# Planned times of TensorE's transposes and products in a two-layer decoder

## The chip, the cores and the metric

The kernel runs on one core of one Trainium2 chip. The metric is the device time of one execution in microseconds (us), of which the median of several runs is taken. A core has TensorE (PE in the profile; its weight loads are PEld), VectorE (DVE), ScalarE (ACT), GpSimd (POOL) and SyncE (SP), which here issues direct DMAs. Each engine works through its own queue in order.

## The reference

Everything is float32. The input x is 16 sequences of 256 tokens with 256 channels: 4096 tokens. Six sublayers follow each other, and each adds to x what it computes from the layer-normalised x:

```python
x = x + _L0_attn_ref(_layernorm(x), ...)           # causal linear attention, 16 heads of 16
x = x + _L0_xattn_ref(_layernorm(x), ctx_1024, ...)  # softmax attention to 77 context rows
x = x + _L0_ffn_ref(_layernorm(x), ...)            # 16 experts, top 2 of a sigmoid router
x = x + _L1_attn_ref(_layernorm(x), ...)           # 8 heads, keys and values of a 64-wide latent
x = x + _L1_xattn_ref(_layernorm(x), ctx_1024, ctx_1024, ..., mask_SxS2_ik0)
x = x + _L1_ffn_ref(_layernorm(x), ...)            # gated, with quantised weights and activations
```

The expert layer gives each expert 640 rows at most and gathers the results of a token's two experts with the router's weights.

## The kernel before, in words

The 4096 tokens are 32 tiles of 128 rows; x stays on chip in 32 tiles of 128x256. Tiles are worked in groups ("batches") of four. The profile shows five stages one after another.

1. `l0_attention` (L520), 0 to 275 us of the span: projections, score products ps_sc, products with the masked scores la_at, and the output product with Wo (ps_av<-w_L_attn_WoT,la_aT).
2. `l0_cross` (L1035), to about 573: for each tile, `scores(i)` makes two pairs of score products (ps_sc). For each pair DVE adds the bias into lx_s and takes the maximum lx_mx, POOL or ACT subtracts it, and ACT takes exponentials. `weighted(i)` transposes the weights (ps_pt, four 128-wide ones twice and then two of 104 columns) and copies them to lx_sT and lx_sL. It multiplies them with the values (ps_rec<-lx_sT,lx_v), scales the result by the reciprocal sums (DVE, lx_aT, L1160) and applies Wo (ps_rec<-w_L_xattn_wo,lx_aT), which DVE adds to x. The scores of tile i+1 are written in the program ahead of the weighted sums of tile i. In between stand the query projections of the batch after next (hT, ps_pr), the keys and values of later batches (ps_k, ps_v), and the expert router of the batch before: the normalised rows rh by ACT, their transposes ps_rt (L832), the logits ps_logit (L839), the top two by DVE, the ranks ps_rank (L879), and scatters of the rows into moe_x by POOL's indirect DMAs.
3. `l0_experts` (L1700), to about 893: products ps_h and ps_y with each expert's weights.
4. `l1_tokens` (L1314), to about 1345: POOL gathers the expert results (ex_yg) by indirect DMA. Then both attentions of layer 1 follow for each tile: scores in two halves of four products, exponentials sa_e, multiplication by the reciprocal sums on POOL, 16 transposes ps_pt, products ps_av with the latent and ps_po.
5. `l1_ffn` (L1920), to the end.

Stages 1 to 4 are not issued in the order of the program text. `planned(E)` (L369) puts a `Plan` in the place of the engines. Each operation is recorded as a `Call` with a planned duration in ns (`busy`) and a delay until its readers may start (`tail`). At the end of a stage, `Plan.issue()` (L149 on) works out an order by list scheduling: of the operations whose inputs are ready in the plan, those that could begin within 150 ns (`near`) of the earliest on an engine compete, and the first in program order (`rank`, shifted where the program says urgent) is taken. A copy made with `nc.copy` goes to VectorE or ScalarE, whichever would finish it first in the plan. TensorE is charged an extra 25 to 205 ns between groups of products that use parts of its rows or columns (`CHANGE`). Then all operations are issued, sorted by planned begin, so that each engine's queue has the planned order; on the chip semaphores enforce what must wait. In the profile every planned operation has line L363, that of `Call.issue`. Stage 5 is not planned and its instructions show lines of their own.

The planned durations are set in `Call.__init__` from the number n of elements in a partition: VectorE 50 + 1.05n (with a tail of 140), ScalarE's copies 45 + 0.83n and activations 170 + 0.73n, POOL by kind (an indirect DMA 1250). TensorE's are the lines that the change touches. A float32 product shows as two matmul records in the profile and a transpose as one.

Of the kernel before, what the change touches and what calls it, by code (L numbers as in the profile page):

```python
# [53 lines left out]
class Plan:  # L54
# [17 lines left out]
    def __init__(self, tc, near=150):  # L72
        self.tc, self.nc, self.near = tc, tc.nc, near
        self.ops, self.tiles, self.open, self.shift = [], {}, None, 0
        self.start, self.gate = 0.0, None
        for name in ("tensor", "vector", "scalar", "gpsimd", "sync"):
            setattr(self, name, Engine(self, name))
# [211 lines left out]
def region(ap):  # L289

    if ap.space == DRAM:
        return ap.tensor.name, 0, 1, 0, 1
    step, rows = ap.ap[0]
    row, first = divmod(ap.offset, step)
    if ap.space == PSUM:
        return ap.tensor.name, row, row + rows, first // 512, first // 512 + 1 + (free(ap) - 1) // 512
    reach = sum(s * (n - 1) for s, n in ap.ap[1:])
    return ap.tensor.name, row, row + rows, first, first + reach + 1


def free(ap):
    n = 1
    for _, k in ap.ap[1:]:
        n *= k
    return n


class Call:
# [3 lines left out]
    def __init__(self, nc, engine, method, args, kwargs, together=False):  # L312
        self.engine, self.method = engine, method
        self.then, self.loose = kwargs.pop("then", None), kwargs.pop("loose", False)
        self.nc, self.args, self.kwargs = nc, args, kwargs
        named = dict(kwargs)
        out = named.pop("out", None)
        rest = list(args)
        if out is None:
            out = rest.pop(0)  # L320
        extra = named.pop("accum_out", None)
        writes = [out] + ([extra] if extra is not None else [])
        reads = []
        for v in rest + list(named.values()):
            if isinstance(v, bass.IndirectOffsetOnAxis):
                v = v.ap
            if isinstance(v, bass.AP):
                reads.append(v)
        self.kind = "all"
        self.writes, self.reads = [region(w) for w in writes], [region(r) for r in reads]  # L330
        n = max(free(a) for a in writes + reads)
        if engine == "tensor":
            self.busy, self.tail = 2 * max(110, 0.84 * free(out)), 220
            if method == "transpose":
                self.busy = max(60, 0.85 * free(out))
            left = reads[0]
            self.part = (left.offset // left.ap[0][0], out.offset // out.ap[0][0])
            if together:
                self.kind = "row" if left.ap[0][1] <= 64 and out.ap[0][1] == P else "col"
        elif engine == "vector":  # L340
            self.busy, self.tail = 50 + 1.05 * n, 140
            if method == "reciprocal":
                self.busy = 145 + 6.35 * n
        elif engine == "scalar":
            self.busy, self.tail = 45 + 0.83 * n, 165
            if method == "activation":
                self.busy = 170 + 0.73 * n + (92 if extra is not None else 0)
        elif method == "indirect_dma_start":
            self.busy, self.tail = 1250, 2000
        elif method == "dma_start":  # L350
            self.busy, self.tail = 60, 2500
        else:
            even = any(s == 0 for r in reads for s, _ in r.ap[1:])
            self.busy, self.tail = (100 + 1.75 * n if even else 200 + 2.0 * n), 95
            if ALU.pow in args:
                self.busy = 970
            elif method == "tensor_scalar":
                self.busy = 50 + 1.2 * n
            elif method == "tensor_copy":
                self.busy = 110 + 1.0 * n  # L360
# [1791 lines left out]
```

## Time and profile before

| what | value |
| --- | --- |
| runs | 1731.65, 1732.46, 1735.03 us; median 1732.46 |
| profiled execution | 1689.03 us, its span 1687.3 us, mean TensorE clock 0.973 |
| TensorE (matmul, weight load) busy | 1555.7 us, 1034.2 us |
| VectorE, ScalarE, GpSimd busy | 1114.1, 769.5, 450.4 us |
| DMA moved | 92.02 MB, mean 55 GB/s |

The busy time of an engine is the union of its instructions' times. A row of a group reads: line, engine, operation, output<-inputs, shapes, count | busy time, mean ns of one | idle time of the engine just ahead of these, and what ended most of it. A window's row reads: the stretch in us from the span's start, its length, then busy time and number of instructions for PE, PEld, DVE, ACT and POOL, the granted TensorE clock (1 is full), the share of DMA engines busy, and GB/s. A row of the waits reads: what waited, for what: us in total, how many times, the longest. A row of a timeline has the start, the length and the instruction (x4: four in a row), with idle time ahead of it in brackets. The profiled execution is shorter than the median of the runs: 1732.46 / 1689.03 = 1.0257.

### The profile page before, as it was taken

How to read it: one execution, taken by the hardware profiler on the slowest of the kernel's cores; microseconds unless marked ns; L12 is line 12 of the kernel's file. 1: busy time of each engine (PE TensorE's matmuls, PEld its weight loads, DVE VectorE, ACT ScalarE, POOL GpSimd, SP SyncE). 2: the span in 40 equal slices, each digit the busy share in tenths (PEclk: the TensorE clock that was granted, in tenths of full speed). 3: DMA queues.
4: the chain of work that ended last, by engine and by line, in shares of the span. 5: the costliest groups of instructions: out<-in, count | busy, mean ns of one | idle time of the engine just before them, and what ended most of it. 6: DMA issues, size and time to landing. Idle time of an engine off the chain costs nothing.

```text
span 1687.3 us, 24347 instructions
## 1 busy us (share of the span) xinstructions
PE 1555.7 (92%) x9072; PEld 1034.2 (61%) x9072; DVE 1114.1 (66%) x2209; ACT 769.5 (46%) x2017; POOL 450.4 (27%) x521
## 2 busy tenths in 40 slices
PE   5999999998997799999997899999999599999799
PEld 3666665665665677777775666666666344433387
DVE  7988886999997442221126788777757543999951
ACT  4333324767767211111113645554555343667850
POOL 5332212355444200000006887343343100000000
PEclk9999999999998899999998999999999799999899
DMA  6024003011111543344312121000000000001111
GB/s 191 1 97 154 1 1 78 16 48 38 34 37 46 169 131 113 112 126 142 115 61 59 51 63 39 1 1 1 1 1 1 0 0 0 25 37 51 38 50 50
DMA packets 95785, 92.02 MB, mean 55 GB/s; under 512 B 32487, under 2 KB 85439, under 8 KB 95667
## 3 DMA queue, kind: packets, MB, share of 16 engines
q1 hardware_dynamic: 89522, 73.91, 14.4%
q0 software_dynamic: 6144, 16.57, 3.1%
q8 instruction: 71, 1.16, 0.3%
q14 instruction: 48, 0.39, 0.1%
HBM read 52.70 MB, written 36.70 MB: 53 GB/s over the span
## 4 chain that ended last, share of the span: by engine, by line
PE 56%; DVE 26%; issue 7%; ACT 7%; DMA 2%; POOL 2%; SPq 1%; POOLq 0%; ACTq 0%; DVEq 0%
PE ps_y L363 7%; PE ps_h L363 7%; PE ps_pr L363 6%; PE ps_av L363 6%; PE ps_gate L486 5%; PE ps_out L486 5%; PE ps_sc L363 4%; PE ps_pt L363 3%; ACT lx_s L363 3%; PE ps_v L363 2%; PE ps_po L363 2%; DVE x L363 2%; DVE lx_mx L363 2%; DVE ff_g L2015 2%; DVE sa_top L363 2%
## 5 line engine op out<-in xcount | busy, mean ns | idle before, releaser
L363 DVE COPY ex_y<-ps_y 128x256 f32<-128x256 f32 x80 | 33.7, 424 | 217.1 <-PE ps_y L363 217.1
L363 POOL DMA_INDIRECT ex_yg<-moe_y,slot x64 | 64.1, 1002 | 337.5 <-DMA moe_y<-ex_y 320.3
L363 POOL TENSOR_TENSOR sa_e<-sa_e,sa_rec 128x1024 f32<-128x1024 f32 x64 | 121.5, 1906 | 121.3 <-PE ps_pt L363 71.3
L486 PE MATMUL ps_up<-ff_x,ffn_up 128*128 128x512 f32 x336 | 147.0, 595 | 7.1 <-DVE ff_pu L1886 4.3
L363 ACT ACTIVATE sa_e<-ps_sc,sa_top 128x256 f32<-128x256 f32 x256 | 118.2, 485 | 72.1 <-DVE sa_top L363 69.9
L363 PE MATMUL ps_y<-w,ex_h 128*128 128x256 f32 x640 | 141.5, 379 | 4.1 <-DVE ex_y L363 4.1
L363 PE MATMUL ps_h<-ex_xT,w 128*128 128x320 f32 x512 | 143.4, 438 | 0.5 <-ACT ex_h L363 0.5
L363 PEld LDWEIGHTS ps_y<-w,ex_h 128*128 128x128 f32 x640 | 121.4, 190 | 23.3 <-DVE ex_y L363 5.3
L363 ACT ACTIVATE ex_h<-ps_h 128x640 f32<-128x640 f32 x64 | 45.0, 704 | 187.0 <-PE ps_h L363 187.0
L363 PEld LDWEIGHTS ps_h<-ex_xT,w 128*128 128x128 f32 x512 | 96.6, 192 | 40.4 <-ACT ex_h L363 1.0
L486 PEld LDWEIGHTS ps_up<-ff_x,ffn_up 128*128 128x128 f32 x336 | 63.0, 190 | 91.0 <-issue 72.9
L363 ACT ACTIVATE lx_s<-lx_s,lx_mx 128x77 f32<-128x77 f32 x288 | 98.9, 347 | 8.4 <-DVE lx_mx L363 4.7
L486 PE MATMUL ps_out<-ffn_down,ff_g 128*128 128x256 f32 x384 | 84.8, 384 | 11.6 <-issue 11.6
L486 PE MATMUL ps_gate<-ff_x,ffn_gate 128*128 128x512 f32 x192 | 85.0, 606 | 6.5 <-DVE ff_x L1988 6.5
L486 PEld LDWEIGHTS ps_out<-ffn_down,ff_g 128*128 128x128 f32 x384 | 74.1, 193 | 22.7 <-issue 12.4
L363 DVE TENSOR_REDUCE sa_top<-ps_sc 128x4 f32<-128x1024 f32 x64 | 76.4, 1215 | 17.1 <-PE ps_sc L363 16.8
L363 DVE TENSOR_TENSOR la_at<-ps_sc,la_tri 128x1024 f32<-128x1024 f32 x64 | 75.8, 1215 | 8.9 <-PE ps_sc L363 8.8
L363 POOL DMA_INDIRECT moe_x<-rh,slot x64 | 63.7, 995 | 41.9 <-issue 14.3
L363 PE MATMUL ps_pt<-ident,sa_e 128*128 128x128 f32 x512 | 66.9, 281 | 5.9 <-ACT ff_x L363 1.9
L363 PE MATMUL ps_sc<-sa_latT,sa_q 64*128 64x256 f32 x512 | 69.9, 399 | 2.3 <-ACT sa_e L363 2.3
L486 PEld LDWEIGHTS ps_gate<-ff_x,ffn_gate 128*128 128x128 f32 x192 | 37.3, 195 | 53.7 <-issue 53.0
L363 PEld LDWEIGHTS ps_pt<-ident,sa_e 128*128 128x128 f32 x512 | 58.9, 144 | 15.1 <-issue 3.2
(301 smaller groups left out, 3402.3 us busy)
## 6 DMA issues: line engine op xcount, KB each, us to landing
w<-in_L_ffn_w SPq DMA_DIRECT2D x32, 512.0 KB
moe_x<-rt_zero SPq DMA_DIRECT2D x16, 640.0 KB
ex_xg<-moe_x SPq DMA_DIRECT2D x15, 640.0 KB
moe_y<-ex_y SPq DMA_DIRECT2D x15, 640.0 KB
x<-in_x SPq DMA_DIRECT2D x32, 128.0 KB
out_x<-x SPq DMA_DIRECT2D x32, 128.0 KB
ff_u<-ff_c SPq DMA_DIRECT2D x6, 512.0 KB
ff_c<-ff_u SPq DMA_DIRECT2D x6, 512.0 KB
```

Source lines behind the costliest of these rows:

```text
L363: made = getattr(getattr(self.nc, self.engine), self.method)(*self.args, **self.kwargs)
L486: E.nc.tensor.matmul(ps, a, b, start=n == 0, stop=n == last)
L2015: nc.vector.scalar_tensor_tensor(gp, low16(gq, I16), sg16, low16(sig, U16), ALU.mult, ALU.mult)
```

## The change

Three numbers in the planned durations of TensorE change. A product is planned at twice max(112, 0.84 times its width) plus 12 ns where it was twice max(110, 0.84 times its width); a transpose at max(70, 1.1 times its width) where it was max(60, 0.85 times its width).

```diff
         if engine == "tensor":
-            self.busy, self.tail = 2 * max(110, 0.84 * free(out)), 220
+            self.busy, self.tail = 2 * max(112, 0.84 * free(out)) + 12, 220
             if method == "transpose":
-                self.busy = max(60, 0.85 * free(out))
+                self.busy = max(70, 1.1 * free(out))
```

Both kernels issue the same operations; the number of instructions on each engine stays within a few, as copies can change between VectorE and ScalarE. Compared as lists, 875 lines of TensorE's order differ, 1625 of VectorE's, 492 of ScalarE's and 406 of GpSimd's; SyncE's is the same. What the order of instructions shows of the places, beside the prediction's steps:

- Stage 2: in batches two to five the two score pairs of a tile stand one behind the other ahead of the two 104-wide transposes, where one pair stood there and one later; one of two 512-wide query projections goes ahead of the weighted sums; ps_rank goes ahead of Wo. The copies of hT: 13 on ScalarE and 1 on VectorE before, 4 and 10 after. Of lx_sT: 40 and 24 before, 49 and 15 after.
- Stage 4: 81 of 128 copies of sa_eT were on ScalarE, now 87; the gathers ex_yg at the stage's start stand in other places among GpSimd's multiplications.
- Stages 1 and 3: orders change, no copy changes its engine.

## The prediction

> **What bounds the kernel now.** I read the page first, then windows cut at the stage borders, then TensorE's waits, then single timelines.
>
> ```profile
> PE 1555.7 (92%) x9072; PEld 1034.2 (61%) x9072; DVE 1114.1 (66%) x2209; ACT 769.5 (46%) x2017; POOL 450.4 (27%) x521
> PE 56%; DVE 26%; issue 7%; ACT 7%; DMA 2%; POOL 2%; SPq 1%; POOLq 0%; ACTq 0%; DVEq 0%
> L363 PE MATMUL ps_pt<-ident,sa_e 128*128 128x128 f32 x512 | 66.9, 281 | 5.9 <-ACT ff_x L363 1.9
> ```
>
> TensorE is busy 92% of the span, yet only 56% of the chain that ended last is its own: a quarter runs over VectorE. The third row matters for the change: a transpose has a mean of 281 ns, but the union of 512 of them is 66.9 us, 131 ns each. Next, the five stages, and five stretches of them:
>
> ```profile
> 0.00:275.00 275.00, 253.61 (x2248) 163.55 (x2248) 223.68 (x343) 99.92 (x195) 83.13 (x127) 0.99 0.24 73
> 275.00:573.00 298.00, 259.01 (x2269) 178.40 (x2270) 255.36 (x728) 201.80 (x791) 134.96 (x190) 0.95 0.17 45
> 573.00:893.00 320.00, 312.89 (x1364) 242.66 (x1365) 81.04 (x178) 53.82 (x82) 1.00 (x2) 0.99 0.39 122
> 893.00:1345.00 452.00, 413.54 (x2282) 275.22 (x2280) 329.51 (x695) 231.10 (x775) 229.53 (x199) 0.96 0.07 19
> ...
> 330.00:500.00 170.00, 157.43 (x1399) 105.85 (x1398) 157.06 (x440) 119.43 (x452) 87.49 (x123) 0.99 0.16 41
> ...
> 980.00:1270.00 290.00, 284.34 (x1568) 184.75 (x1567) 217.47 (x463) 152.14 (x512) 139.71 (x116) 0.99 0.05 14
> ```
>
> The columns after the length are TensorE, weight loads, DVE, ACT, POOL, clock. TensorE idles 21.4 us in stage 1 (linear attention), 39.0 in stage 2 (cross attention), 7.1 in stage 3 (experts), 38.5 in stage 4 (layer 1 attentions); all that an order can win is in there. In the middle of stage 2 TensorE and DVE are equally full (157.4 and 157.1 of 170), so each waits for the other; in the middle of stage 4 TensorE alone is full (284 of 290). The waits of stage 2:
>
> ```profile
> PE ps_rec L363 <- DVE lx_aT L363: 9.6, 11, 2.1
> PE ps_xT L363 <- DMA ex_xg<-moe_x: 8.5, 1, 8.5
> PE ps_rt L363 <- ACT rh L363: 4.6, 2, 4.2
> ...
> PE ps_pt L363 <- ACT lx_sT L363: 2.9, 4, 0.8
> ```
>
> The costliest is the output product (Wo) of a token tile, which waits for DVE's lx_aT.
>
> **The change, part by part.** No instruction is added or removed. Planned costs of TensorE go up: a 128-wide transpose from 108.8 to 140.8 ns (max(60, 0.85·128), max(70, 1.1·128)), a product by 12 to 16 ns (256 wide: 430 to 442). What happens on the chip is a new order, and some copies on the other engine. Are the new figures nearer the trace?
>
> ```profile
> 1105.76 0.59 PE L363 MATMUL ps_pr<-hT,sa_aq 128*128 128x512 f32 x1
> 1106.18 1.91 PE L363 MATMUL ps_pt<-ident,sa_e 128*128 128x128 f32 x16
> 1107.98 0.48 PE L363 MATMUL ps_cv<-cx_v,cx_eT 77*128 77x256 f32 x1
> ```
>
> From the first of 16 transposes to the instruction behind them is 1.80 us, 112.5 ns each. The Trainium skill ("TensorE: Matmul & The Clock Gate", PE-mode transpose) gives about 275 ns for a 128x128 transpose in a kernel, which this trace's mean of 281 ns repeats; by that figure even 141 is short, 16 would hold TensorE 4.4 us, and the change would be a step to the truth. By the row they hold it 1.80 us, because they overlap; the planner adds its costs end to end, so the cadence is what it needs, and 108.8 was within 4% of it while 140.8 is 25% above. I take the row. For products the old figures also fit: four 256-wide ones started 1.73 us before what follows them (432 each), two 512-wide ones 1.72 us (860). So TensorE is now planned too slow, while DVE stays planned too fast (a 616-wide add at 50 + 1.05·616 = 697 ns against 790 in the trace). The plan thinks that DVE is further ahead than it is.
>
> Stage 2, five full batches of four tiles. A batch lasted 34.7 us (from router logits to router logits: 36.2, 34.9, 34.9, 34.3, 33.4). Before, around one of the Wo products:
>
> ```profile
> 428.60 0.60 PE L363 MATMUL ps_pt<-ident,lx_s 128*128 128x128 f32 x4
> 430.03 0.43 PE L363 MATMUL ps_pt<-ident,lx_s 128*104 128x128 f32 x2 [0.83 <-ACT lx_sT L363]
> ...
> 431.69 1.98 PE L363 MATMUL ps_pr<-hT,w_L_xattn_wq 128*128 128x512 f32 x4
> 433.73 1.13 PE L363 MATMUL ps_rec<-w_L_xattn_wo,lx_aT 128*128 128x256 f32 x4
> ```
>
> - The score pairs move ahead of the two 104-wide transposes and cover that 0.83 (seen three times: 0.5 a batch). The Wo at the batch's end moves behind the 8 transposes of rh and covers its wait for lx_aT (2.10, 1.46 and 0.49 us in three batches: 0.8 a batch). A third, between the last two transposes, covers 0.2.
> - Against it: with the two score pairs so early, DVE has two pairs of add and maximum ahead of lx_aT where it had one: 2 · 0.79 = 1.6 us later. TensorE is there earlier, as one of the two 512-wide products (0.86) now stands ahead of the weighted sums, and the waits of this stretch grow from about 1.1 to about 3.1 us: +2.0 a batch. Behind this Wo in TensorE's queue stand the next tile's transposes, all idle for that time; DVE waits for nobody meanwhile. The rh transposes, reached before the Wo, wait 0.5 for ACT.
> - Nine of 14 hT copies and three of lx_sL move to DVE, thirteen others from DVE to ACT: DVE's load changes by about −1 us over the stage. I cost this at nothing, as ACT has 50 of 170 us free; if DVE is late by one 0.69 us copy at each batch, it is +0.7 a batch.
>
> Sum: 2.0 + 0.5 − 0.5 − 0.8 − 0.2 = +1.0 a batch, +5 over five. Bounds: no new Wo wait, −1.5 a batch (−7.5); all of it and the copy, +1.7 (+8.5). At the stage's end a Wo goes behind both score pairs instead of between them; its tile ends about 1 us later, but ACT's exponentials feed the next step anyway: +0.5 (−0.5 to +1.5).
>
> Stage 1: in seven places the Wo product goes ahead of the scores instead of behind. It saves a change of row grouping (this Wo takes 1.06 us behind scores, 0.86 to 0.90 elsewhere: −0.2) and waits for la_aT about as long (+0.2). 0, between −2 and +2. Stage 3: only weight and input transposes swap, TensorE at 98%: 0 ± 1.
>
> Stage 4: in five places the first half of a tile's score products moves from between transposes to its second half (one change less: −0.2 each, −1.0). Their softmax is needed a tile later, some 8 us, which hides it; without that cover each would cost up to a scores-to-exponentials delay of 1 to 2 us. At the start (893 to 980, TensorE 71.9 of 87, POOL 68.8) POOL's gathers of expert results move ahead of softmax multiplications; a gather is 1.0 us of POOL, so two or three of them make these 2 to 3 us later, and the tiles that need the gathers earlier by the same. No row shows which is late next; I take +1 between −3 and +4. SP's queue is the same. Stage 5 is not planned: 0.
>
> Total: 5 + 0.5 + 0 + 0 − 1 + 1 = +5.5 us on the profiled execution of 1689.03 (span 1687.3), 1694.5. The median of the runs is 1732.46, 1.0257 times that; scaled, 1738.1 us.
>
> **Rivals.** *The covered waits win.* The Wo wait behind the logits stays at its old length, because TensorE gets there later than I walked it; then a batch gains 1.5 and stage 4 one: −8.5, 1680.5, scaled 1723.7. For it: those waits are in the table. Against: DVE is as full as TensorE, so a wait covered here comes back there. It decides at a Wo wait that grows by less than 1.0 us a batch.
> *All is hidden.* Order changes, DVE's 157 us a stretch stay, and each batch ends when DVE does: 1732.5, within 3. For it: equal loads. This is also the case that the change doesn't do what it says, as the new costs are no nearer.
> *DVE and POOL both late.* +8.5 in stage 2, +1.5 at its end, +4 at the start of stage 4, +2 in stage 1: +16, scaled 1748.9. For it: POOL and DVE each have an underestimated plan; against: four ends at once.
>
> **How the numbers follow.** My forecast (+2 to +10 profiled, likeliest 1738.1) 0.46; hidden 0.26; waits win 0.19; both late 0.09. A measurement of this kernel can tell about 0.2%, 3.5 us, from no change. Most of the forecast and the last rival lie above it, the edges go to "same": faster 0.18, same 0.29, slower 0.53. The range runs from 1725 (short of the winning case's centre) to 1750 (the late case): the part outside is at most half of the first rival and of the last.
>
> **What would show it.** In the trace after: the wait of ps_rec for lx_aT grows from 9.6 to some 16 us with single waits of 2 us or more behind ps_rank, while ps_pt's wait for ACT lx_sT falls under 1; the batches last 35 to 36.5 us; stage 4's middle stays at 290 less one; stages 3 and 5 keep their lengths. I am wrong if the batches come under 34 us, or if the difference sits at the start of stage 4.

## The result, and the profile after

The changed kernel takes 1778.68 us (median of 4 runs, 1772.77 to 1788.86); beside it the kernel before takes 1732.06. The ratio is 1.0257, 95% interval 1.023 to 1.0284: 2.6% slower, where 1738.1 was forecast. The profiled execution took 1773.76 us, its span is 1772.0. Of the page and of windows cut at its own stage borders, the lines that answer to those of before:

```profile
PE 1584.8 (89%) x9072; PEld 1047.1 (59%) x9072; DVE 1110.9 (63%) x2203; ACT 772.1 (44%) x2023; POOL 450.9 (25%) x521
...
PE 52%; DVE 26%; issue 8%; ACT 8%; another core or an unknown queue 3%; DMA 2%; POOL 1%; SPq 0%; POOLq 0%; ACTq 0%; DVEq 0%
```

```profile
0.00:278.00 278.00, 256.36 (x2250) 164.68 (x2250) 224.38 (x344) 100.05 (x195) 84.59 (x129) 0.99 0.23 72
278.00:643.00 365.00, 277.65 (x2268) 189.51 (x2268) 254.18 (x726) 202.31 (x792) 134.38 (x187) 0.86 0.14 37
643.00:962.00 319.00, 312.08 (x1358) 241.87 (x1359) 80.93 (x178) 53.06 (x81) 0.05 (x1) 0.99 0.38 123
962.00:1430.00 468.00, 422.30 (x2287) 276.78 (x2286) 327.03 (x690) 233.94 (x781) 230.11 (x200) 0.96 0.07 19
1430.00:1772.00 342.00, 316.43 (x912) 174.24 (x912) 224.43 (x266) 182.78 (x175) 1.79 (x5) 0.97 0.09 31
```

Stage 2 has grown from 298 to 365 us and stage 4 from 452 to 468; the others keep their lengths within 3 us. DVE does the same work in stage 2 (254 us), in a longer time. Most of the growth there is one kind of wait, which TensorE's table names only at second hand (ps_rec for lx_aT, 46.4 us). ScalarE's waits in stage 2, and the timelines of TensorE and ScalarE at the first of them, show it:

```profile
ACT lx_rT L363 <- remote: 56.3, 7, 11.8
```

```profile
338.28 0.38 PE L363 MATMUL ps_rec<-lx_sL,lx_v 104*32 104x128 f32 x2
...
336.03 0.59 ACT L363 COPY lx_sT<-ps_pt 128x512 f32<-128x512 f32 x1
348.46 0.37 ACT L363 COPY lx_rT<-ps_rec 128x256 f32<-128x256 f32 x1 [11.84 <-remote]
```

The copy lx_rT needs what TensorE wrote into ps_rec, and the last of those products had started before 338.6. The copy starts at 348.5, and the profile knows no releaser ("remote"). I call waits without a known releaser freezes. This profile has one more of VectorE (x, 4.2 us); the profile of before has none. Each of the eight begins while GpSimd issues the scatters of a batch (the first at 336.6; scatters from 334.5 to 346.3). In three of the sets of runs below the kernel before takes 1690, and no profile has a freeze; in two others, as in the runs above, it takes 1732 to 1741, and every profile of a kernel that issues the scatters has them. One chip was met in both conditions. So the two profiles shown of before and after come from different conditions, while the ratio of 1.0257 is of runs side by side.

### The profile page after: what moved, and what is told of

It reads as the page before. It is cut to its first block, busy times and chain, and to the rows that moved or that the text cites. A ratio compares the mean times of both kernels' runs of the same rounds, so it can differ in the third digit from the quotient of the medians.

```text
span 1772.0 us, 24370 instructions
## 1 busy us (share of the span) xinstructions
PE 1584.8 (89%) x9072; PEld 1047.1 (59%) x9072; DVE 1110.9 (63%) x2203; ACT 772.1 (44%) x2023; POOL 450.9 (25%) x521
## 4 chain that ended last, share of the span: by engine, by line
PE 52%; DVE 26%; issue 8%; ACT 8%; another core or an unknown queue 3%; DMA 2%; POOL 1%; SPq 0%; POOLq 0%; ACTq 0%; DVEq 0%
PE ps_y L363 7%; PE ps_h L363 7%; PE ps_gate L486 5%; PE ps_out L486 5%; PE ps_av L363 5%; PE ps_pr L363 4%; PE ps_sc L363 4%; PE ps_pt L363 3%; DVE la_rec L363 3%; ACT lx_s L363 3%; PE ps_rec L363 2%; DVE la_at L363 2%; PE ps_v L363 2%; PE ps_po L363 2%
## 5 line engine op out<-in xcount | busy, mean ns | idle before, releaser
L363 PE MATMUL ps_rec<-w_L_xattn_wo,lx_aT 128*128 128x256 f32 x128 | 41.2, 450 | 50.5 <-DVE lx_aT L363 46.4
```

The source lines that it names most:

```text
L363: made = getattr(getattr(self.nc, self.engine), self.method)(*self.args, **self.kwargs)
```

## The experiments

Every ratio is to the kernel before, run on the same chip in the same set.

**First set: which stage, and the freezes.** The first is the kernel before unchanged. The next two give the new costs to the plans of some stages only. The fourth keeps the changed order and doesn't issue GpSimd's scatters of rows into moe_x, so that the experts work on zeros.

```diff
-def planned(E):
+def planned(E, raised=False):        # sets Call.raised while the stage is recorded
-    with ExitStack() as ctx, planned(E) as nc:
+    with ExitStack() as ctx, planned(E, True) as nc:   # in l0_cross, or in the three others
```

```diff
-        made = getattr(getattr(self.nc, self.engine), self.method)(*self.args, **self.kwargs)
+        if self.then is None or self.method != "indirect_dma_start": made = getattr(...)
```

> The kernel before, unchanged (one blank line more). Two theories of the 43 us between its profiled execution (1689) and the median of its runs (1732). Freeze theory: TensorE's results reach ScalarE's copy lx_rT late (seven waits of 5 to 11 us while GpSimd's scatters moe_x<-rh run, in the profile of the changed kernel); the usual run of before has some of these too, so a profile with 1730 us shows three to five waits of ScalarE lx_rT for something the profile cannot name, some 40 us in all, in stage 2. Scale theory (mine): the whole execution is 1.026 times longer, at a lower clock, evenly in all stages. Time: 1731 by both.

> The new costs in the plan of stage 2 alone; stages 1, 3 and 4 in the order of before. If the whole loss is in stage 2 (70 us of the 85 between the two profiles): 1765 to 1785 us, with the freezes. If the loss is spread over the stages: 1740 to 1755.

> The new costs in the plans of stages 1, 3 and 4; stage 2 in the order of before. If the loss is stage 2's: 1732 to 1742 us, of which stage 4's start may hold some. If spread: 1750.

> The changed kernel's order without issuing GpSimd's 64 scatters moe_x<-rh (moe_x stays zero, so the experts work on zeros; their time is the same). Freeze theory: the seven waits of lx_rT for an unnamed releaser go, and the time falls by 55 to 85 us against the changed kernel, to 1690 to 1725. If it is the order alone (waits for DVE): the waits for lx_aT stay at some 46 us, and the time falls by under 15 us.

Measured: before 1690.86 (15 runs) and again 1690.39, ratio 1.000 (0.9986 to 1.0014), no freeze: the condition was another than that of the result, and neither theory of the 43 us between profile and runs could be tried on before itself. The new costs in stage 2 alone: 1701.1, 1.0058 (1.0036 to 1.008). In the others: 1701.63, 1.0077 (1.0054 to 1.0099). Neither profile has a freeze. The loss is in stage 2 and in stage 4, about evenly. Without scatters the changed order took 1700.33, 1.0063 (1.0046 to 1.008); as no kernel froze here, the run doesn't bear on the freezes.

**Second set: the change again, and its two halves.** The changed kernel and the kernel before unchanged, and each of the two costs raised alone.

```diff
-                self.busy = max(60, 0.85 * free(out))
+                self.busy = max(70, 1.1 * free(out))                            # tr_only
-            self.busy, self.tail = 2 * max(110, 0.84 * free(out)), 220
+            self.busy, self.tail = 2 * max(112, 0.84 * free(out)) + 12, 220     # prod_only
```

> The changed kernel once more (a blank line more), beside the kernel before on one chip. In the first experiments before ran at 1691, the new costs in stage 2 alone cost 11.7 us in the traces and in the other stages 8 to 9. If the two simply add and the freezes of the recorded run belong to that chip and not to the order: 1708 to 1714 where before is at 1691, no wait of lx_rT for an unnamed releaser. If the freezes belong to the order of the whole: 1770 again, with before at 1690.

> The kernel before, for a profile on this chip. If before is at 1690 here: no freeze. If it is at 1732: three to five freezes of ScalarE's lx_rT in stage 2, by the freeze theory, while the other stages keep their lengths within 1 us.

> Only the transpose's planned cost is raised (109 to 141 ns), the product's left. My theory has the transposes as the part that overshoots, 25% above the cadence: it should cost most of the loss, 10 to 20 us over before on the same chip. Rival: each change of order is a draw of its own, and either part alone costs between 0 and 20.

> Only the product's planned cost is raised (430 to 442 ns for 256 columns). By my theory within 2 to 3% of the cadence either way, so little: 0 to 6 us. By the rival (any change of order draws anew): as much as the transposes alone, 5 to 20.

Measured: before 1690.49, its profiled run 1691.05; the change 1717.49, ratio 1.0148 (1.0112 to 1.0183), without a freeze. So the order alone costs 27 us (25 by the ratio), and the freezes belong to the condition, not to the order of the whole. Transposes alone: 1704.8, 1.0085 (1.0055 to 1.0114), a little over half of it. Products alone: 1700.75, 1.0055 (1.0037 to 1.0072), more than the 0 to 6 that I gave them. Together they cost about what they sum to. The profile of this run of the changed kernel is the one to lay beside that of before, as neither has freezes: TensorE's waits in stage 2,

```profile
PE ps_rec L363 <- DVE lx_aT L363: 9.2, 18, 1.8
PE ps_pt L363 <- DVE hT L363: 5.6, 5, 1.3
PE ps_pr L363 <- DVE lx_k L363: 5.0, 4, 1.4
```

and two stretches of TensorE's timeline, with VectorE's copies of keys (lx_k) at the second:

```profile
425.12 0.43 PE L363 MATMUL ps_pt<-ident,lx_s 128*104 128x128 f32 x2 [1.33 <-DVE hT L363]
...
435.57 1.31 PE L363 MATMUL ps_sc<-lx_k,lx_q 64*128 64x308 f32 x8
436.81 0.43 PE L363 MATMUL ps_pt<-ident,lx_s 128*104 128x128 f32 x2
438.39 1.13 PE L363 MATMUL ps_pr<-hT,w_L_xattn_wq 128*128 128x512 f32 x2 [1.16 <-DVE lx_k L363]
...
437.51 0.83 DVE L363 TENSOR_SCALAR lx_k<-ps_k,lx_sel 128x154 f32<-128x154 f32 x2
```

Both waits are for a buffer in PSUM, the memory that TensorE writes its results to, and not for data. ps_ht, ps_pt, ps_k, ps_pr and others share a ring of three in this stage. The transposes want the one that DVE's hT copies empty, and the query projection one of ps_k, which DVE has read at 438.34, behind the router's work. The batches last 35.96, 37.10, 37.17, 36.31 and 37.22 us, 36.75 on average, against 34.73 in the profile of before of this set (from router logits to router logits). In stage 4, the same two profiles at the start of the stage, first before, then after:

```profile
958.70 0.66 PE L363 MATMUL ps_pt<-ident,sa_e 128*128 128x128 f32 x4 [0.85 <-DVE x L363]
959.28 1.13 PE L363 MATMUL ps_sc<-sa_latT,sa_q 64*128 64x256 f32 x8
960.35 1.94 PE L363 MATMUL ps_av<-sa_eT,sa_lat 128*64 128x512 f32 x8
```

```profile
973.29 0.66 PE L363 MATMUL ps_pt<-ident,sa_e 128*128 128x128 f32 x4 [2.48 <-DVE x L363]
973.88 2.07 PE L363 MATMUL ps_sc<-sa_latT,sa_q 64*128 64x256 f32 x8
975.88 2.64 PE L363 MATMUL ps_av<-sa_eT,sa_lat 128*64 128x512 f32 x8
```

The same transposes wait 1.6 us longer for a DVE addition to x, and the products behind them then take 2.07 and 2.64 us where they took 1.13 and 1.94. VectorE and GpSimd after:

```profile
968.85 3.60 DVE L363 TENSOR_SCALAR h<-x,ln_mv,ln_rstd 128x256 f32<-128x256 f32 x1
972.83 0.41 DVE L363 TENSOR_TENSOR x<-x,ps_po 128x256 f32<-128x256 f32 x1
...
968.53 3.76 POOL L363 TENSOR_TENSOR sa_e<-sa_e,sa_rec 128x1024 f32<-128x1024 f32 x2
```

The addition is that of ps_po, which again frees a PSUM buffer (four in this stage). It is late because h<-x ahead of it took 3.60 us, and ends 0.16 us after two softmax multiplications of GpSimd, which the new order has back to back behind two gathers. This h<-x takes 0.41 us as a rule. In the two traces 13 of 192 take 1.5 to 3.6 us, and each of the 13 ends 0.15 or 0.16 us after such a multiplication that it overlaps. So the multiplications seem to hold it; no run tried it.

The windows of 6 us there (958 to 964 before, 973 to 979 after) have the granted clock in the last column but two:

```profile
958.00:964.00 6.00, 5.30 (x31) 2.95 (x32) 4.58 (x8) 4.91 (x19) 5.41 (x4) 1.00 0.25 70
```

```profile
973.00:979.00 6.00, 5.71 (x26) 2.79 (x28) 3.30 (x8) 4.11 (x16) 3.88 (x4) 0.72 0.23 68
```

From the start of the wait to the instruction behind ps_av (at 962.22 and 978.45) are 4.4 us before and 7.6 after: a wait that is 1.6 us longer here costs 3.3.

**Third set: undo one wait, and dose the transpose's cost.** The first gives the ten hT copies of stage 2 that the changed plan puts on VectorE to ScalarE, at their places in the order (nine of them were there before the change). The second moves the first half of the query projection back behind the weighted sums. The last two are before with another cost of a transpose: 120 and 100 ns for 128 columns.

```diff
+        if op.choice and op.writes[0][0].startswith("hT"): op.calls = op.both[1:]   # after_hT_act
+        order.insert(j - 1, order.pop(i))      # after_wq_back: i, j the halves of one ps_pr
-                self.busy = max(60, 0.85 * free(out))
+                self.busy = max(66, 0.94 * free(out))     # tr_120
+                self.busy = max(56, 0.78 * free(out))     # tr_100
```

> The changed kernel's order, with the nine hT copies of stage 2 that it gives to VectorE given to ScalarE instead, each at the same place in the order. In the trace of the changed kernel (1714.5 us span) TensorE waits 5.6 us in stage 2 for hT on VectorE, since the next transposes need the PSUM buffer. Buffer theory: that wait falls under 1 us and the batches shorten by 0.5 to 1.1 us each: 3 to 5 us less than the changed kernel (1717 where before is 1690). Rival (ScalarE is then late with its exponentials, or VectorE was the bound anyway): within 2 us of it or slower.

> The changed kernel's order on all engines, but the first half of the 512-wide query projection goes back behind the weighted sums, next to its second half (as before the change). Buffer theory: its wait for VectorE's lx_k (5.0 us in four batches, for the PSUM buffer of ps_k) falls under 1 us, and of it 2 to 4 us are gained. My prediction's theory (with the projection there, Wo waits less for lx_aT): the wait for lx_aT falls by about the same, and more is gained, 4 to 8 us. Rival: the wait moves to the next thing that VectorE owes, gain under 1.5 us.

> Only the transpose's planned cost, raised a third of the way: 120 ns for 128 columns (109 before, 141 in the change), which is the cadence with small gaps (120 ns in stage 4's middle). If a cost near the cadence is best: 1686 to 1694 where before is 1690, and under tr_only (1705). If any change of order draws anew: between 1690 and 1710, with no trend over 100, 109, 120, 141.

> The transpose planned too fast: 100 ns for 128 columns, 10% under the cadence. If the loss comes from overshooting (waits for PSUM buffers that the plan doesn't see): no such loss on this side, 1686 to 1696. If any error of the cost or any change of order costs alike: 1698 to 1710.

Measured, before at 1690.38. hT on ScalarE: 1721.5, 1.0183 (1.0163 to 1.0202), no gain. TensorE's waits in its stage 2:

```profile
PE ps_pt L363 <- ACT hT L363: 6.7, 5, 1.6
```

The wait has changed its engine and is longer, and the batches last 38.3 us, 1.6 more than in the change. Projection back: 1715.31, 1.0158 (1.0133 to 1.0183), no gain that shows against 1.0148; its batches last 36.8. Its wait for lx_k is gone, but that for lx_aT is 11.1 us (9.2) and one of 4.3 us for ScalarE's lx_sL is new. Both theories that looked at single waits fell here: taking one away moves it. The dose fared better: 120 ns gave 1701.47, 1.0069 (1.0052 to 1.0087), four fifths of the loss of the whole step to 141; 100 ns gave 1686.51, 0.9978 (0.9966 to 0.999), faster than before. By their profiles this is a trend in stage 2 alone, taken from its first ps_sc to the first ps_h: 306.9 us at 100 ns, 306.9 to 308.0 in three profiles of before, 311.1 at 120, 315.8 at 141. Stage 4 is 458.6, 459.6 to 459.8, 465.8 and 462.0.

That led to a packing theory: with TensorE planned too slow, the plan sets what needs a PSUM buffer or a DVE result closer behind TensorE's work than the others can deliver. Then it is the relation of the costs that decides.

**Fourth set: the relation, or a draw for each order.**

```diff
+                self.busy = max(62, 0.875 * free(out))    # tr_112
+                self.busy = max(50, 0.7 * free(out))      # tr_90
+            self.busy, self.tail = 2 * max(106, 0.81 * free(out)), 220          # both_low, with
+                self.busy = max(56, 0.78 * free(out))                           # this
+            self.busy, self.tail = 1.2 * (50 + 1.05 * n), 140   # after_rest_slow: the new costs, and
+            self.busy, self.tail = 1.2 * (45 + 0.83 * n), 165   # VectorE, ScalarE 1.2 times as long
...                                                      # (ScalarE's activations too)
```

> The transpose planned at 112 ns for 128 columns, the measured cadence, where before has 109 and tr_120 has 120 (1701 where before is 1690). If the relation of costs decides, smoothly: 1688 to 1695. If each order is a draw: anywhere from 1684 to 1706.

> The transpose planned at 90 ns, 20% under the cadence, everything else as before. Packing theory: TensorE looks faster than it is, the plan keeps other work between a transpose and what needs its PSUM buffer, so no loss: 1682 to 1692. Draw theory: 1684 to 1706.

> Transposes planned at 100 ns as in tr_100 (1686.5) and products lower too, 415 ns for 256 columns where before has 430. Packing theory: as good as tr_100 or better, 1680 to 1690. Draw theory: 1684 to 1706.

> TensorE's costs as in the change, and VectorE's and ScalarE's planned durations 1.2 times as long. Packing theory: the plan again sees the waits for those engines and keeps work in between; most of the 27 us comes back, 1690 to 1702. Draw theory or a theory in which absolute times matter: no better than the changed kernel, 1705 to 1725.

Measured: before takes 1741.09 here (36 runs), so the condition is that of the result, and only ratios are compared. 112 ns: 1.005 (1.003 to 1.007). 90 ns: 0.9969 (0.9953 to 0.9985). Both low: 0.9896 (0.9863 to 0.9929). New costs with the other engines slower: 1.0048 (1.0033 to 1.0063), against 1.0257 (1.023 to 1.0284) of the change in this condition. By planning the other engines slower too, four fifths of the change's loss come back by the ratios (0.0257 to 0.0048), as the packing theory had it; the draw theory had no reason for it. But 112 ns loses 0.5% for a step of 3%, more than a smooth law gives, so a part of each result is the draw of an order. Nor is all of these ratios order: all four profiles have freezes, and not equally many. ScalarE's waits for no named releaser at lx_rT, first with 112 ns, then with both low:

```profile
ACT lx_rT L363 <- remote: 38.2, 7, 7.2
```

```profile
ACT lx_rT L363 <- remote: 9.7, 2, 7.0
```

With both low, five such waits of VectorE come to it (15.5 us); 90 ns has 22.8 us; and in after_rest_slow all kinds make 43.5 us, against 60.5 in the profile of the change.

Nearly all of them lie in stage 2, so the rest of the span (without the stretch from its first ps_sc to the first ps_h) can be compared over the conditions, by one profile each:

| kernel | span without stage 2, us | stage 2, us |
| --- | --- | --- |
| before, three profiles | 1380 to 1383 | 307 to 308, no freezes |
| the change | 1394 and 1397 | 321 without freezes, 375 with |
| after_rest_slow | 1382 | 371, freezes |
| both_low, both_low_2 | 1374 and 1376 | 344 and 346, freezes |
| 90 ns | 1383 | 353, freezes |
| 112 ns | 1388 | 351, freezes |

Outside stage 2, after_rest_slow wins back the 12 to 15 us that the change loses there. In stage 2 it is about as long as the change, both with freezes, so whether its order is better there wasn't seen. Of 90 ns no gain shows outside the stage with the freezes. A difference of some us is weak: the changed order without scatters takes 1391 there in one profile and 1399 in another.

**Fifth set: what was left.**

> both_low once more. Where before is at 1690 (no freezes): packing theory 1678 to 1688, a gain of its own; if its gain was only fewer freezes, 1688 to 1694. Where before is at 1732 to 1741: 1722 again.

> The changed kernel's order without issuing the 64 scatters (moe_x stays zero, so the experts work on zeros). Where before is at 1732 to 1741: if the scatters are needed for the freezes, no wait of lx_rT for an unnamed releaser and 1700 as on the other chip; if not, 1760 with the waits. Where before is at 1690: 1700 again, which tells nothing new of this.

Measured, before at 1735.35. both_low: 1723.61, 0.9916 (0.9886 to 0.9946): again faster than both kernels, but again in the condition with freezes; its profile has 25.1 us of them, 13.1 for ScalarE's lx_rT and 12.0 for DVE's. Outside stage 2 it gains 4 to 8 us on before; what it takes in all without freezes wasn't seen. The changed order without scatters: 1707.85, 0.9824 (0.9785 to 0.9862), no freeze in the profile, its batches as in the first set within 0.1 us for the first five (34.98, 36.54, 35.71, 34.85, 34.77). With scatters the same order takes 1778.68 beside a before of 1732. So the freezes need GpSimd's scatters. By what they act isn't shown: without them GpSimd also has 64 us less to do, and the order was 17 us shorter even where nothing froze (1700.33 against 1717.49).

## Why the prediction failed

I forecast +5.5 us for the new order; the runs without freezes show +27. What failed is the sum of stage 2, the sum of stage 4 and the scaling.

**The direction and its ground were right.** I took the row (a transpose every 112.5 ns) over the Trainium skill's 275 ns ("TensorE: Matmul & The Clock Gate", PE-mode transpose) and concluded that 141 overshoots. The doses without freezes agree: 100 ns is faster than before (0.9978), 120 and 141 are slower (1.0069, 1.0085). By the skill's figure 141 would have been nearest the truth. In the condition with freezes 90 ns is faster (0.9969) and 112, the cadence itself, slower (1.005); as the table shows, the first may be fewer freezes, and the second is one order, so what cost is best stays open.

**"DVE stays planned too fast" was wrong.** I set 697 ns of plan against a duration of 790 in the trace, having just refused that for TensorE. By starts, in the timeline of VectorE before,

```profile
413.75 0.78 DVE L363 TENSOR_REDUCE lx_mx<-lx_s 128x8 f32<-128x616 f32 x1
414.45 0.79 DVE L363 TENSOR_TENSOR lx_s<-ps_sc,lx_bias 128x616 f32<-128x616 f32 x1
```

a 616-wide instruction is followed by the next after 0.70 us: the plan had it right.

**Stage 2: the failed term.** I gave it +1.0 us a batch, of which +2.0 was a longer wait of Wo for lx_aT. Measured is +2.0 a batch (36.75 against 34.73), from elsewhere: lx_aT stayed at 9.2 us (9.6 before, I expected some 16). The gain that I credited for ScalarE's lx_sT came. New are 5.6 us for hT and 5.0 for lx_k, together 2.1 a batch, both of them for PSUM buffers. I had priced hT's copies "at nothing, as ACT has 50 of 170 us free": I asked which engine has room, and not when the copy frees the buffer that TensorE's next instruction needs. The wait of the query projection that goes ahead, for the buffer of ps_k, stands nowhere in my sum. That these two waits are the +2.0 is read from the trace. after_hT_act and after_wq_back took away VectorE's part in the one and all of the other, and neither gained, so what holds a batch at 36.75 stays open. My bound for "no new Wo wait" was wrong too: the sum without the 2.0 is −1.0 a batch, not −1.5, and the first rival rests on it.

**Stage 4: the step with the wrong sign.** I put the moved score products at −1.0 us and their cover at nothing, and the start at +1. In the second set the stage grew by 11.4 us (from the last ps_y to the first ps_gate, 459.6 before and 471.0 after; 469 to 476 in other profiles of this order). With the same instructions (ps_po) laid side by side, after lies 13.5 us behind where the stage starts, 20.4 at 1066 us of before, 26.7 at 1282 and 24.9 at the end. So some 7 come at the start, 6 in the middle, and 2 go again.

At the start I bounded what GpSimd's new order does at +4. I left out that VectorE's h<-x waits, by the times above, until those multiplications end, and the lower clock behind TensorE's wait. The lower clock comes again 65 us on: waits of 2.27 and 1.10 us, 1.51 and 1.10 before, and then twelve transposes hold TensorE 2.62 us instead of 1.37. In the middle, TensorE now waits before the ninth transpose of 16 for the buffer that hT's copy frees, here in the same tile before and after:

```profile
1134.02 1.96 PE L363 MATMUL ps_pt<-ident,sa_e 128*128 128x128 f32 x16
```

```profile
1157.59 1.04 PE L363 MATMUL ps_pt<-ident,sa_e 128*128 128x128 f32 x8
1158.88 1.15 PE L363 MATMUL ps_pt<-ident,sa_e 128*128 128x128 f32 x8 [0.26 <-ACT hT L363]
```

By the starts the pause is 0.42 to 0.46 us over the cadence, in two of 14 tiles before and in seven after: 2.2 us. Two new waits of 1.02 us for DVE's x make 2.0, and 3.4 us at half the clock behind the first of them most of the rest. That the moved score products used to cover these waits is argued, not shown; in the tile above they had not moved. The change of row grouping was saved, as I said, at 0.2 us (two halves of score products take 1.06 and 1.07 us apart, 1.93 together).

**The scale was no scale.** I multiplied by 1.0257, the median of the runs over the profiled execution, as if it lay over the whole time. (That the measured ratio is 1.0257 too is chance.) It was a condition in which before takes 42 us more, and the profile that I had showed none of it. That condition and this order together account for the rest of the miss: without freezes the change costs 27 us, in the condition with freezes 46.6. That the freezes are longer in this order (56 us in its profile) than in that of before was not seen in a profile of before, as none fell into this condition; it is argued from the two ratios.

**The rivals.** "All is hidden" and "the covered waits win" are out. "DVE and POOL both late" was nearest: it had the start of stage 4 and twice my stage 2, and gave 1748.9; its size without freezes, +16, is still short of +27.

**Left open:** what holds a batch of stage 2, why TensorE's results reach the others late while GpSimd issues scatters in one condition and not in the other, and how much of both_low's gain is its order.

## What to carry to other kernels

A list scheduler needs costs from start to start; durations of pipelined instructions, put end to end, make the engine look slow. The plan then seems to place what needs its buffers too close: planning the other engines slower as well won the loss back outside stage 2. But each new order is also a draw of some us, so a single run of a new cost proves little. Before pricing a moved instruction at nothing, ask which buffer it gave time to be emptied, not only whose data it waits for. If the runs and the profile differ by more than their scatter, find out what the difference is before scaling with it.

## What was not expected of the hardware

- In one condition, waits for results that TensorE had begun long before, in every profile of a kernel that issues indirect scatters from GpSimd (4.0 to 11.8 us in the change, 1.8 to 7.5 for lx_rT in the others), and none in the order without scatters (after_noscatter_2). In the same order stage 2 is 365 us long with freezes and 310 without (278 to 643, and 278 to 588 in after_again).
- After a wait of 2.48 us the granted clock was 0.72 over 6 us (0.50 from 973.9 to 977.3), after one of 0.85 us it was 1.00, so the 1.6 us more cost twice that. It isn't a matter of one wait's length alone: waits of 1.02 and 0.76 us close together are followed by 3.4 us at 0.50 at 1103.6, and by 1.00 at 1208.
- VectorE's h<-x (128x256, 0.41 us) takes 1.5 to 3.6 us where it runs beside GpSimd's multiplication sa_e, and ends 0.15 us after it. An addition with an operand in PSUM (x<-x,ps_po) isn't held: 0.42 us at 948.91 of before_third, within a multiplication from 947.74 to 949.64.
